# Layer 0 of a graph network on Trainium2: the next layer's projection moved between weighing and y2's product, and y1 transposed from its two parts

## The chip, the core and the metric

The kernel runs on one core of a Trainium2 chip. The metric is the time of the whole program on the device in microseconds (us). Its median of three runs before the change is 1384.36 us (1383.07 to 1384.51).

## What is computed

Four layers with residual and layer normalisation over x of shape (8, 2048, 64) and a 2048 x 2048 matrix `adj` whose rows are 0 or one constant. The change concerns layer 0 and the first step of layer 1:

```python
# layer 0
w = einsum('nd,dkio->nkio', embedding, weight)      # 16 x 3 x 64 x 64 weight, one mix per node
As = [I, A, 2 A A - I]                              # K = 3
x_g = einsum('knm,bmc->bnkc', As, x)
out = einsum('bnki,nkio->bno', x_g, w) + embedding @ bias
x = layernorm(x + out)
# layer 1, first steps
h = x @ W
s = leaky_relu(h @ a_node, 0.2)
alpha = softmax(where(H.T > 0, s, NEG))
agg = einsum('ben,bnf->bef', alpha, h)
... x @ W_ind ...                                   # the other half of the projection
```

## The kernel before

The 2048 nodes are 16 tiles of 128; a tile holds 128 nodes by 512 columns (8 batches by 64 features). A stage ahead of layer 0 computes y1 = A x for all tiles and keeps it as two parts, `y_hi` (rounded to fp32r) and `y_lo` (the rest), because two fp32r products replace a full fp32 one.

`layer0` then runs a loop over j = 0 to 16, with eight groups g in each pass. The order on each engine is the order in which the code is written: `program_order` ties the instructions of PE (TensorE), DVE (VectorE), ACT (ScalarE) and POOL (GpSimd) one behind the other. The steps of a pass are:

- `weigh(j, g)` (L1010): PE multiplies the transposed terms x, y1, y2 of tile j with a slice of the weights into a tile `pp` of PSUM, 24 instructions; DVE drains it in four steps (L1031), which scale by the embedding and add to the residual `r`. The pool `ps_p` holds two such tiles, so weigh g needs that DVE has drained weigh g-2.
- `normed(j-1, 0..2)` (L1035) at g = 0, 1, 2: layer normalisation of the tile before, on DVE and ACT.
- `scaled(j+1, h)` (L931) and `compare` (L946): POOL and DVE check the mask of the next tile against the matrix; `mask(j+2, h)` makes the masks of the one after.
- `first_terms(j+1)` (L953) at g = 2: POOL adds `y_hi` and `y_lo` to y1 (L956); PE transposes it in four pieces with the identity (L959, listed under the helper's line L152); ACT copies the result. Then the bias product `bp` and the residual.
- `product(j+1)` (L978) at g = 3: y2's product, 32 matmuls with the mask. Behind it `to_features(j-1)` transposes the normalised tile to `xT1` (`trx`).
- `second_term(j+1)`, `scores(j-1)` and `gather(j-2)` at g = 6; the gather adds to `aggp` the product of `mds` (memberships) and `hss` (projected features times scores).
- `degrees(j+1)` (`dgp`, L1005) and `project(j-1)` (L1091) at g = 7. The projection takes a `pp` tile too (named `hp`): 8 products (16 instructions on PE), two ACT copies (L1115, L1116), a DVE subtraction (L1117) and POOL's product `hs` (L1124). It ends a pass, and the next instruction of PE is weigh(j+1, 0).

Pass 16 has no weighing left: it finishes tile 15, gathers tile 14, spreads the memberships over four SBUF tiles (`spread`, L1131), sums the softmax denominators (`denp`, L1144, 16 products) and gathers tile 15. Several tiles live in the homes (numbered buffers) of a pool `own`, which the stage before has left.

Of the kernel before, what the change touches and what calls it, by code (L numbers as in the profile page):

```python
# [8 lines left out]
F32 = mybir.dt.float32  # L9
# [37 lines left out]
def r_(ap):  # L47
    return ap.bitcast(F32R)
# [3 lines left out]
def kernel(  # L52
# [31 lines left out]

    ident = const.tile([P, P], F32, tag="ident", name="ident")
    make_identity(nc, ident)
    ones = const.tile([P, P], F32, tag="ones", name="ones")
    nc.vector.memset(ones, 1.0)
    eps_t = const.tile([P, 1], F32, tag="eps", name="eps_t")
# [61 lines left out]
    def transpose(dst, src):  # L151
        nc.tensor.matmul(dst, src, ident, start=True, stop=True, is_transpose=True)  # L152
# [727 lines left out]
    def layer0(  # L880
# [7 lines left out]
        raws, msk, terms, resid, norm, srow = {}, {}, {}, {}, {}, {}  # L888
        x1s, xTs, hps, hss, mds = {}, {}, {}, {}, {}

        homes = {"xT": (0, 1, 2), "xs": (3, 4), "y1": (5,), "y1T": (6, 7), "r": (8, 9),
                 "y2": (10,), "y2T": (11, 12), "cs": (13, 14), "sq": (15,)}
        turn = {}

        def tile(tag, name, shape=(P, BC), bufs=2):
            if tag not in homes:
                return l0s.tile(list(shape), F32, tag=tag, name=name, bufs=bufs)
            turn[tag] = turn.get(tag, -1) + 1
            home = homes[tag][turn[tag] % len(homes[tag])]
            return own.tile(list(shape), F32, tag=f"b0_{home}", name=name)  # L900
# [51 lines left out]

        def first_terms(j):  # L953

            y1 = tile("y1", f"y1_{j}")
            nc.gpsimd.tensor_tensor(y1, y_hi[:, j, :], y_lo[:, j, :], ALU.add)  # L956
            tr = ps_tr.tile([P, NP, P], F32, tag="tr", name=f"try1_{j}")
            for pr in range(NP):
                transpose(tr[:, pr, :], y1[:, pr * P:(pr + 1) * P])  # L959
            y1T = tile("y1T", f"y1T_{j}", (P, NP, P))  # L960
            nc.scalar.copy(y1T, tr)
            terms[j]["y1"] = y1T
            bp = ps_tr.tile([P, QW], F32, tag="tr", name=f"bp_{j}")
            nc.tensor.matmul(bp[:, 0:C], terms[j]["et"], bias_sb, start=True, stop=True)
            bn = tile("bn", f"bn_{j}", (P, C))
            nc.scalar.copy(bn, bp[:, 0:C])
            r = tile("r", f"r0_{j}")
            for bq in range(2):
                nc.gpsimd.tensor_tensor(
                    r[:, 4 * bq * C:4 * (bq + 1) * C]  # L970
                    .rearrange("p (h l c) -> p h l c", h=2, l=2),
                    swapped(terms[j]["xs"], bq),
                    bn.rearrange("p (h l c) -> p h l c", h=1, l=1).to_broadcast([P, 2, 2, C]),
                    ALU.add,
                )
            resid[j] = r
# [114 lines left out]
        def project(j):  # L1091

            mm = ps_p.tile([P, 2, 2, 4 * C], F32, tag="pp", name=f"hp_{j}")
            mm = mm.rearrange("p h l (m x) -> p h (l m) x", m=2)
            for pr in range(NP):
                for h in range(2):
                    rs = slice(h * 64, (h + 1) * 64)
                    nc.tensor.matmul(  # L1098
                        mm[:, h, pr, :], xTs[j][rs, pr, :], wb[rs], start=True, stop=True
                    )  # L1100
            if j < NT - 1:
                md = tile("md", f"md_{j}", (P, 2, E))
                nc.gpsimd.tensor_copy(md, pm[:, j, :].unsqueeze(1).to_broadcast([P, 2, E]))
                mds[j] = md.rearrange("p h e -> p (h e)")

            def by_half(t):
                return t.rearrange("p (r h c) -> p h r c", h=2, c=C)


            stay = j >= len(kept_i)  # L1110
            if stay:
                hi, lo = y_hi[:, j, :], y_lo[:, j, :]
            else:
                hi, lo = (tile(k, f"{k}_{j}", bufs=1) for k in ("ihi", "ilo"))
            nc.scalar.copy(r_(by_half(hi)), mm[:, :, :, C:2 * C])  # L1115
            nc.scalar.copy(by_half(h_sb[:, j, :]), mm[:, :, :, 0:C])  # L1116
            nc.vector.tensor_tensor(  # L1117
                r_(by_half(lo)), mm[:, :, :, C:2 * C], by_half(hi), ALU.subtract
            )
            if not stay:  # L1120
                for t, kept_part in zip((hi, lo), kept_i[j]):
                    nc.sync.dma_start(kept_part, t)
            hss[j] = tile("hs", f"hs_{j}", bufs=1)
            nc.gpsimd.tensor_tensor(  # L1124
                b_view(hss[j]), b_view(h_sb[:, j, :]), bcast(es[:, j, :]), ALU.mult
            )

        def gather(j):
            nc.tensor.matmul(aggp, mds[j], hss[j], start=j == 0, stop=j == NT - 1)  # L1129

        def spread():  # L1131

            mds.clear()
            for q, home in enumerate((1, 2, 3, 5)):
                md = own.tile([P, 4, 2, E], F32, tag=f"b0_{home}", name=f"md4_{q}")
                nc.gpsimd.tensor_copy(
                    md, pm[:, 4 * q:4 * q + 4].unsqueeze(2).to_broadcast([P, 4, 2, E])
                )
                for t in range(4):
                    mds[4 * q + t] = md[:, t].rearrange("p h e -> p (h e)")  # L1140

        def denominators(lo, hi):
            for j in range(lo, hi):
                nc.tensor.matmul(  # L1144
                    denp[0], mds[j], es[:, j, :], start=j == 0, stop=j == NT - 1
                )
# [19 lines left out]
        with program_order():  # L1166
            first_terms(0)
            scaled(0, 0)
            scaled(0, 1)
            for _ in product(0):  # L1170
                pass
            second_term(0)
            for j in range(NT + 1):
                first = j == 0
                if not first:
                    when(j + 2, load_adj)
                when(j + 2, load_x)
                for g in range(8):
                    when(j, weigh, g)
                    if g == 0:  # L1180
                        when(j - 1, normed, 0)
                        if first:
                            compare(0, 0)
                            compare(0, 1)
                            load_adj(2)
                    elif g == 1:
                        when(j - 1, normed, 1)
                        if j == NT:
                            denp.append(ps_acc.tile([P, BC], F32, tag="acc", name="denp")[:, 0:B])
                            gather(NT - 2)  # L1190
                            spread()
                            denominators(0, NT - 1)
                        if first:
                            degrees(0)
                        when(j + 1, scaled, 0)
                    elif g == 2:
                        when(j - 1, normed, 2)
                        when(j + 1, first_terms)
                    elif g == 3:
                        if j + 1 < NT:  # L1200
                            for _ in product(j + 1):
                                pass
                        when(j - 1, to_features)
                        when(j + 1, compare, 0)
                        when(j + 1, scaled, 1)
                        if j == NT - 2:
                            for t in range(len(kept_i)):
                                for y, kept_part in zip((y_hi, y_lo), kept_i[t]):
                                    nc.sync.dma_start(y[:, t, :], kept_part)
                        when(j + 2, mask, 0)  # L1210
                        when(j + 2, mask, 1)
                    elif g == 5:
                        when(j + 1, compare, 1)
                        if j:
                            next(flags, None)
                    elif g == 6:
                        when(j + 1, second_term)
                        when(j - 1, scores)
                        if j < NT:
                            when(j - 2, gather)  # L1220
                        else:
                            denominators(NT - 1, NT)
                            nc.vector.tensor_scalar(rden, denp[0], TINY, None, op0=ALU.max)
                            nc.vector.reciprocal(rden, rden)
                    elif g == 7:
                        when(j + 1, degrees)
                        when(j - 1, project)
            gather(NT - 1)


# [811 lines left out]
```

## Time and profile before

| what | busy us | share of the span |
|---|---|---|
| PE | 1308.3 | 95% |
| PEld (weight loads, overlapping PE) | 1025.6 | 74% |
| DVE | 929.7 | 67% |
| POOL | 442.3 | 32% |
| ACT | 363.8 | 26% |

| stage | from, us | to, us |
|---|---|---|
| y1's product | 7 | 150 |
| layer 0's loop | 150 | 742 |
| layer 1 | 742 | 1062 |
| layers 2 and 3 | 1062 | 1384 |

How to read the profile: a line of the timeline gives the start, the duration of a merged group of like instructions, the engine, the line of the kernel, the operation, the tile written and those read, the shape and the count; square brackets give how long the engine stood idle before it and which work released it. A line of waits gives who waited for whom, the total in us, how often, and the longest. An "issue" is time in which an engine waited for nothing that the profile shows. An fp32 matmul appears as two instructions; fp32r as one.

### The profile page before, as it was taken

Reading aid. Unit: us, or ns where it says so; the run is one execution under the profiler, and the core shown is the slowest. Engines: PE = TensorE matmul, PEld = TensorE weight load, DVE = VectorE, ACT = ScalarE, POOL = GpSimd, SP = SyncE. Lnnn points to the kernel's source line nnn. Section 1 sums busy time; section 2 is a strip of 40 time slices with the busy share of each in tenths; the row PEclk is TensorE's granted clock in tenths of the full one; section 3 lists DMA queues with packets and bytes.
Section 4 is the critical chain, followed back from the end, with each engine's and each line's share of the span. In section 5 each row is a group of like instructions: output and inputs, shape, how many; then the busy total and the mean of one; then the engine's idle time right before and its main releaser. Section 6 shows DMA issues by size and latency. Waiting matters only on the chain.

```text
span 1383.9 us, 19824 instructions
## 1 busy us (share of the span) xinstructions
PE 1308.3 (95%) x7692; PEld 1025.6 (74%) x7692; DVE 929.7 (67%) x1658; ACT 363.8 (26%) x844; POOL 442.3 (32%) x372
## 2 busy tenths in 40 slices
PE   7999889999999999999986799999997899999997
PEld 6777678888888888888875466666665688888885
DVE  5555347787777777777672678888885666566554
ACT  3000101212222111211221346665655321111111
POOL 0000443444444444444410345665653320000000
PEclk9999989999999999999995599999999899999999
DMA  9765323333323333221603121222220223333552
GB/s 311 215 184 173 128 95 102 102 102 102 99 93 98 103 102 101 98 98 62 218 27 114 61 79 75 76 77 76 77 76 1 92 72 116 117 122 138 184 188 71
DMA packets 91047, 153.00 MB, mean 111 GB/s; under 512 B 12097, under 2 KB 55489, under 8 KB 84673
## 3 DMA queue, kind: packets, MB, share of 16 engines
q1 hardware_dynamic: 88642, 147.46, 31.7%
q10 hardware_dynamic: 2304, 4.20, 0.8%
q8 instruction: 63, 1.03, 0.3%
q14 instruction: 38, 0.31, 0.1%
HBM read 115.97 MB, written 35.66 MB: 110 GB/s over the span
## 4 chain that ended last, share of the span: by engine, by line
PE 81%; DVE 3%; issue 2%; ACT 1%; POOL 1%; POOLq 0%; ACTq 0%; DVEq 0%
PE pp L1020 24%; PE a L1288 17%; PE ind L1288 9%; PE y2p L983 9%; PE fc L798 2%; PE u L1371 2%; PE df L807 2%; PE gp L693 2%; PE try L152 1%; PE yp L1400 1%; PE aggp L1129 1%; PE trm L152 1%; PE tr_l L152 1%; DVE r L1031 1%; PE hp L1098 1%
## 5 line engine op out<-in xcount | busy, mean ns | idle before, releaser
L1031 DVE SCALAR_TENSOR_TENSOR r<-pp,emb_sb,r 128x256 f32<-128x256 f32 x512 | 247.3, 483 | 134.3 <-PE pp L1020 119.7
L1020 PE MATMUL pp<-w_sb,xT 64*128 64x256 f32 x1024 | 163.1, 391 | 11.8 <-PE hp L1098 10.3
L1020 PE MATMUL pp<-w_sb,y1T 64*128 64x256 f32 x1024 | 156.7, 378 | 0.0
L1020 PE MATMUL pp<-w_sb,y2T 64*128 64x256 f32 x1024 | 156.6, 378 | 0.0
L1020 PEld LDWEIGHTS pp<-w_sb,xT 64*128 64x128 f32 x1024 | 98.2, 187 | 34.6 <-issue 15.1
L469 PE MATMUL y1p<-x_hi,m 128*128 128x512 f32 x256 | 106.2, 415 | 7.2 <-ACT x_hi L417 7.2
L734 POOL TENSOR_TENSOR ez<-ez,coef 128x1024 f32<-128x1024 f32 x32 | 65.1, 2033 | 141.2 <-DVE ez L732 141.2
L1020 PEld LDWEIGHTS pp<-w_sb,y1T 64*128 64x128 f32 x1024 | 104.1, 188 | 7.8
L1020 PEld LDWEIGHTS pp<-w_sb,y2T 64*128 64x128 f32 x1024 | 104.1, 188 | 7.9
L1288 PE MATMUL ind<-y_hi,mj_l 128*128 128x512 f32 x256 | 106.6, 417 | 1.0 <-DVE dlt L763 0.8
L983 PE MATMUL y2p<-y_hi,msk 128*128 128x512 f32 x256 | 103.7, 405 | 0.0
L1288 PE MATMUL a<-y_hi,mj_l 128*128 128x512 f32 x256 | 102.4, 400 | 0.0
L983 PE MATMUL y2p<-y_lo,msk 128*128 128x512 f32 x256 | 101.7, 397 | 0.0
L1288 PE MATMUL a<-y_lo,mj_l 128*128 128x512 f32 x256 | 101.6, 397 | 0.0
L469 PE MATMUL y1p<-x_lo,m 128*128 128x512 f32 x256 | 101.4, 396 | 0.0
L1288 PE MATMUL ind<-y_lo,mj_l 128*128 128x512 f32 x256 | 101.1, 395 | 0.0
L1288 PE MATMUL a<-v_hi,mj_l 128*128 128x512 f32 x256 | 100.1, 392 | 0.0
L1288 PE MATMUL a<-v_lo,mj_l 128*128 128x512 f32 x256 | 100.0, 391 | 0.0
L1124 POOL TENSOR_TENSOR hs<-h,es 128x512 f32<-128x512 f32 x16 | 16.7, 1044 | 246.3 <-ACT h L1116 222.3
L935 POOL TENSOR_TENSOR ms<-msk,srow 128x1024 f32<-128x1024 f32 x32 | 77.4, 2420 | 7.5 <-DVE ms L948 5.3
L1288 PEld LDWEIGHTS ind<-y_hi,mj_l 128*128 128x128 f32 x256 | 48.6, 190 | 33.7 <-issue 19.1
L948 DVE SCALAR_TENSOR_TENSOR ms<-ms,adj 128x1024 f32<-128x1024 f32 x32 | 63.9, 1998 | 0.0
(262 smaller groups left out, 2434.3 us busy)
## 6 DMA issues: line engine op xcount, KB each, us to landing
mj_l<-mask SPq DMA_DIRECT2D x48, 1024.0 KB, 4.9
raw<-in_at SPq DMA_DIRECT2D x32, 512.0 KB, 4.8
adj<-in_at SPq DMA_DIRECT2D x64, 256.0 KB, 3.3
mask<-msk SPq DMA_DIRECT2D x32, 512.0 KB, 3.1
xraw<-in_xn SPq DMA_DIRECT2D x8, 512.0 KB, 5.4
oh<-oh SPq DMA_DIRECT2D x16, 256.0 KB, 3.4
xT<-in_xt SPq DMA_DIRECT2D x16, 256.0 KB, 2.9
xs<-in_xn SPq DMA_DIRECT2D x16, 256.0 KB, 2.6
```

What stands on the lines that cost most here:

```text
L152: nc.tensor.matmul(dst, src, ident, start=True, stop=True, is_transpose=True)
L469: nc.tensor.matmul(accs[q][jj], r_(m[:, t, jj * P:(jj + 1) * P]), r_(part[:, mt, :]), start=i + h + t == 0 and part is x_hi, stop=i == 3 a ...
L693: nc.tensor.matmul(gp[:, u, :], r_((oh01, oh23)[i][rs, cols]), r_(part[rs]), start=part is agg_hi, stop=part is agg_lo,)
L734: nc.gpsimd.tensor_tensor(by_b(ez), by_b(ez), per_b(coef, 2 * i, 2), ALU.mult)
L798: nc.tensor.matmul(fc[:, h, :], fcw_sb[rs], sT[rs], start=True, stop=True)
L807: nc.tensor.matmul(df[:, b:b + 1], th[:, b % 2, (b // 2) * P:(b // 2 + 1) * P], av_sb, start=True, stop=True,)
L935: nc.gpsimd.tensor_tensor(ms, m, srow[j].unsqueeze(1).to_broadcast([P, 8, P]), ALU.mult)
L948: nc.vector.scalar_tensor_tensor(ms, ms, 1.0, raws[j][h], op0=ALU.mult, op1=ALU.not_equal, accum_out=bad[:, 2 * j + h:2 * j + h + 1],)
L983: nc.tensor.matmul(acc, r_(msk[j, mt // 8][:, mt % 8, :]), r_(part[:, mt, :]), start=mt == 0 and part is y_hi, stop=mt == NT - 1 and part ...
L1020: nc.tensor.matmul(pp[:, h, pl, :], terms[j][name][rs, 2 * bq + pl], w_sb[rs, k, dq * 4 * C:(dq + 1) * 4 * C], start=k == 0, stop=k == K - 1,)
L1031: nc.vector.scalar_tensor_tensor(rb, ppv[:, :, dd, :], emb_sb[:, j, d:d + 1], rb, op0=ALU.mult, op1=ALU.add)
L1288: nc.tensor.matmul(acc, r_(a[:, mt, :]), r_(part[:, mt, :]), start=mt == 0 and part is hi, stop=mt == NT - 1 and part is lo,)
```

## The change

The projection of tile j-2 is now issued at g = 3, after weigh(j, 3) and ahead of y2's product, instead of the projection of tile j-1 at the end of the pass. It is meant to have its PSUM tile drained while the product runs. In pass 16 the projection of tile 14 comes at g = 3, that of tile 15 after the loop, and gather(14) moves from g = 1 to g = 6, behind the last denominators. `hss` therefore lives in home 5, which y1 leaves, and `spread` uses home 10 in place of 5; in the last two projections the membership tile is taken from `spread`.

y1 is no longer summed by POOL: PE multiplies each of the two parts with a rounded identity and adds both in PSUM, 8 products of 128 x 128 by 128 in fp32r instead of 4 transposes in fp32.

```diff
     make_identity(nc, ident)
+    ident_r = const.tile([P, P], F32, tag="ident_r", name="ident_r")
+    nc.vector.tensor_copy(r_(ident_r), ident)
...
-        homes = {"xT": (0, 1, 2), "xs": (3, 4), "y1": (5,), "y1T": (6, 7), "r": (8, 9),
+        homes = {"xT": (0, 1, 2), "xs": (3, 4), "hs": (5,), "y1T": (6, 7), "r": (8, 9),
...
         def first_terms(j):
-            y1 = tile("y1", f"y1_{j}")
-            nc.gpsimd.tensor_tensor(y1, y_hi[:, j, :], y_lo[:, j, :], ALU.add)
             tr = ps_tr.tile([P, NP, P], F32, tag="tr", name=f"try1_{j}")
             for pr in range(NP):
-                transpose(tr[:, pr, :], y1[:, pr * P:(pr + 1) * P])
+                for part in (y_hi, y_lo):
+                    nc.tensor.matmul(
+                        tr[:, pr, :], r_(part[:, j, pr * P:(pr + 1) * P]), r_(ident_r),
+                        start=part is y_hi, stop=part is y_lo,
+                    )
...
-            if j < NT - 1:
+            if j not in mds:
                 md = tile("md", f"md_{j}", (P, 2, E))
...
-            for q, home in enumerate((1, 2, 3, 5)):
+            for q, home in enumerate((1, 2, 3, 10)):
...
                         if j == NT:
                             denp.append(ps_acc.tile([P, BC], F32, tag="acc", name="denp")[:, 0:B])
-                            gather(NT - 2)
                             spread()
                             denominators(0, NT - 1)
...
                     elif g == 3:
+                        when(j - 2, project)
                         if j + 1 < NT:
                             for _ in product(j + 1):
                                 pass
...
                             denominators(NT - 1, NT)
+                            gather(NT - 2)
                             nc.vector.tensor_scalar(rden, denp[0], TINY, None, op0=ALU.max)
...
                     elif g == 7:
                         when(j + 1, degrees)
-                        when(j - 1, project)
+            project(NT - 1)
             gather(NT - 1)
```

## The prediction

> **What bounds the kernel now.** I read the page's busy shares and its chain first, then PE's waits in layer 0 (200 to 740 us), then the timeline of one pass.
>
> ```profile
> PE 1308.3 (95%) x7692; PEld 1025.6 (74%) x7692; DVE 929.7 (67%) x1658; ACT 363.8 (26%) x844; POOL 442.3 (32%) x372
> ...
> PE 81%; DVE 3%; issue 2%; ACT 1%; POOL 1%; POOLq 0%; ACTq 0%; DVEq 0%
> ```
>
> TensorE sets the time: it is 95% busy and carries 81% of the chain that ended last. An edit counts by what it does to PE's queue. What PE waits for in layer 0:
>
> ```profile
> PE pp L1020 <- PE hp L1098: 10.3, 13, 0.8
> ...
> PE pp L1020 <- DVE r L1031: 1.4, 2, 1.1
> ```
>
> The first is one wait of 0.79 us in each of 13 passes, put down to the projection `hp`. The timeline, PE first, then DVE:
>
> ```profile
> 446.90 0.38 PE L1005 MATMUL dgp<-ones,cs 128*128 128x1 f32 x2
> 447.21 1.16 PE L1098 MATMUL hp<-wb,xT 64*128 64x128 f32 x16
> 449.16 0.70 PE L1020 MATMUL pp<-w_sb,xT 64*128 64x256 f32 x4 [0.79 <-PE hp L1098]
> ```
>
> ```profile
> 447.02 2.04 DVE L1031 SCALAR_TENSOR_TENSOR r<-pp,emb_sb,r 128x256 f32<-128x256 f32 x4 [1.56 <-PE pp L1020]
> 449.57 0.69 DVE L1117 TENSOR_TENSOR ilo<-hp,ihi 128x512 fp32r<-128x512 f32 x1 [0.51 <-ACT h L1116]
> ```
>
> `hp` is done by 448.37, yet weigh(j+1, 0) starts at 449.16, 0.10 after DVE has drained weigh 7 at 449.06. `pp` has two buffers and `hp` takes one of them (weigh 6's), so weigh(j+1, 0) must wait for weigh 7's. The releaser is DVE, not `hp`. A pass takes 35.07 us from one degree product to the next; in it DVE is busy 26.5 us (busy time by window), so DVE is second.
>
> [...] the trace has 108 to 109 ns between loads. [...] the comparison (L948) takes 3.00 us while GpSimd is at work, 1.22 us while it is idle.
>
> **The change part by part.**
>
> *The projection's place.* Same matmuls, ACT copies and DVE subtraction. At pass end, weigh(j+1, 0) now follows the degree product at 447.21 and takes weigh 6's buffer, which DVE released at 444.6: the wait is gone. At the new place, after weigh 3, `hp` takes weigh 2's buffer. PE's 1.2 us for `hp` are added there and leave the pass end: sum nothing. Behind it in PE's queue stands y2's product (32 matmuls), which uses no `pp`; the copies and the subtraction (0.59 + 0.59 + 0.69) lie under its 7.45 us. Weigh 5, which needs `hp`'s buffer, is some 10 us later. So gone are 13 x 0.79 = 10.3 us, plus 1.1 at 237 us (the first such pass, booked under DVE): **-11.4 us**.
>
> *Does another wait take its place?* With weigh(j+1, 0) at 447.21 and 2.6 us per weigh: weigh 1 at 449.87 needs weigh 7's buffer (449.06: free); weigh 2 at 452.47 needs weigh 0's (matmuls done 450.1, drained 2.04 us later, 452.15: free by 0.3); weigh 3 at 456.8 needs weigh 1's (normed's 1.4 us stand between, so 455.6: free); `hp` at 459.5 needs weigh 2's (458.1: free). None, but the slack at weigh 2 is small. On DVE the subtraction now precedes the comparison and two masks (at most 3.0 + 2.9 us), ahead of weigh 4's drain; DVE stood idle 2.96 us before that drain, and `hp` gives PE 1.2 us more, so it is hidden.
>
> *GpSimd.* `hs` no longer keeps scaled(j+1, 0) waiting 14.79 us for ACT; the sum of y1 (1.27 us, L956) goes. It ended at 422.02 and the transposes began at 422.07, so at most 0.05 us per pass was on the path; I count nothing. `hs` now delays scaled(j+1, 1) by about 2 us; its user, the comparison, comes 15.4 us after the product's start: hidden.
>
> *y1's transposes.* Per pass 4 transposes become 8 fp32r products of 128x128 by 128. Before, 4 take 0.59 us to the next operation:
>
> ```profile
> 422.07 0.66 PE L152 MATMUL try<-ident,y 128*128 128x128 f32 x4
> 422.66 0.43 PE L964 MATMUL bp<-bias_sb,et 16*128 16x64 f32 x2
> ```
>
> They start 0.11 us apart. No run of them in fp32r is in the trace, but a single one of the same shape is, between 512-column products:
>
> ```profile
> 144.07 0.19 PEld L390 LDWEIGHTS sm<-S,rk 128*128 128x128 f32 x1
> 144.30 0.22 PE L390 MATMUL sm<-S,rk 128*128 128x128 f32 x1
> 144.36 0.45 PE L469 MATMUL y1p<-x_hi,m 128*128 128x512 f32 x1
> ...
> 144.64 0.39 PE L469 MATMUL y1p<-x_lo,m 128*128 128x512 f32 x1
> ```
>
> From 144.30 to 144.64 are 0.34 us, where one product alone takes 0.23: the short one costs 0.11, a weight load. I take 0.11. The lower bound is 0.06 (the distance to its successor), the upper 0.23 (a 512-column product). At 0.11: 4 more x 0.11 = 0.44 per pass, x 15 = **+6.6 us** (upper: 8 x 0.23 - 0.44 = 1.4, x 15 = 21). The first tile's are at 150.5 us at half clock (4 took 1.08): +0.85, of which 0.45 falls into the bias product's wait for a DMA: **+0.4**.
>
> *End of the layer.*
>
> ```profile
> 719.40 1.06 PE L1098 MATMUL hp<-wb,xT 64*128 64x128 f32 x16
> 722.75 1.13 PE L1129 MATMUL aggp<-hs,md 128*128 128x512 f32 x2 [2.29 <-POOL hs L1124]
> 723.72 6.17 PE L1144 MATMUL denp<-es,md 128*128 128x8 f32 x30
> 729.74 1.09 PE L152 MATMUL trx<-ident,x 128*128 128x128 f32 x4
> ...
> 735.28 0.60 PE L1144 MATMUL denp<-es,md 128*128 128x8 f32 x2 [1.42 <-ACT es L1089]
> ```
>
> The gather, queued ahead of the denominators, waits 2.29 us for `hs`. Afterwards the denominators start at 719.7 (`md` is spread early: its homes are free) and, still at full clock (0.11 each), end at 723, the projection of tile 14 at 724.3. Then trx waits for x1 of tile 15, which comes at 726.5 (before 727.2; the 0.69 us subtraction is no longer ahead): 3.2 us earlier than 729.74. But gather(14) now stands behind the last denominator and ahead of the last projection: 2.05 us at half clock (as L1129 at 740.18), 1.03 at full. I take half and round up for the extra copies and the table loads: **-1.7** here (-0.7 to -2.7; were all at full clock, some -3).
>
> *Small.* The copy of the identity lies in DVE's first wait for a load (3.79 us): nothing. The chain for `dinv` (L1324 on), which DVE works off at 693 to 696 while it waits, would hold up weigh 0's drain about 0.9 us in one pass, more than the slack of 0.3: **+0.4**. Layers 1 to 3 are untouched.
>
> Sum: -11.4 + 6.6 + 0.4 - 1.7 + 0.4 = -5.7, so 1384.4 - 5.7 = **1378.7 us**.
>
> **The rivals.** (a) *A wait in the place of the old one.* DVE's drain (2.04 us a weigh plus normed) becomes what ends last at weigh 2 or 3, and the loop keeps its 35.07 us. For: the slack of 0.3, and PE already waited 0.32 once (703.06). Against: DVE has 8 us free in a pass. Only the end of the layer gains: 1384.4 + 0.4 - 1.7 = 1383.1. (b) *The short products are dear.* At 0.23 each: -11.4 + 21 + 1 - 1.7 + 0.4 = +9.3, 1393.7, slower. For: they have never been run back to back here. Against: L390's 0.11, in 12 of its 16 places. (c) *The end gains more*, if the clock holds through the last scores and gathers: some 3 us more than in the sum, 1375.7.
>
> **How the numbers follow.** My case 0.62, (a) 0.14, (b) 0.08, (c) 0.16. The time is the first's. The range reaches (c) and (a) and a price of 0.16 for a short product (+0.05 x 8 x 15 = 6): 1374.5 to 1384.5. 0.2% is 2.8 us: my case and (c) are faster, less a part of my case in which a slightly higher price leaves under 2.8: faster 0.76, same 0.15, slower 0.09.
>
> **What would show it.** Right: passes of about 34.75 us; no wait of `pp` at pass ends; `hp` starting 0.3 us after weigh 3; the eight short products in about 0.9 us; `aggp` last ending about 1.7 us earlier against the end of weigh(15, 7). Wrong: a wait of `pp` on DVE at weigh 1 to 3, the short products above 0.15 us apart, y2's product waiting behind `hp`, or the comparison taking 3.0 us where it took 1.22.

## The result, and the profile after

The changed kernel takes 1367.32 us (median of four runs), the kernel before beside it 1383.80 us: ratio 0.9878, 95% interval 0.9859 to 0.9897. The gain is 16.5 us, where 5.7 were predicted and 1374.5 was the low end of the range. One of the four runs (1393.83) had a lower clock (0.946, against 0.966 to 0.968 in the others) and is not in the ratio. The profiled executions stand 19.8 us apart (spans 1383.9 and 1364.1), 3.3 us more than the medians: the one before took 1385.91 us, 2.1 above its median, the one after 1366.07, 1.25 below. The stages below are from these two, one execution each.

The page of the kernel after: busy shares, and shares of the chain that ended last.

```profile
PE 1306.2 (96%) x7756; PEld 1021.9 (75%) x7756; DVE 929.9 (68%) x1659; ACT 364.5 (27%) x844; POOL 420.4 (31%) x355
...
PE 83%; DVE 3%; ACT 1%; issue 1%; POOL 0%; ACTq 0%; POOLq 0%; DVEq 0%
```

PE still sets the time and has hardly less to do (1308.3 us busy before); what went is time in which it waited, as the stages below show. PE's waits in layer 0 after (160 to 735 us), with the lines that answer to those of before:

```profile
PE aggp L1133 <- POOL hs L1128: 2.3, 1, 2.3
PE pp L1024 <- DVE r L1035: 1.7, 3, 1.1
```

The 13 waits of `pp` put down to `hp` are gone. The timeline of PE after, at a pass's end and at the projection's new place:

```profile
435.76 0.38 PE L1009 MATMUL dgp<-ones,cs 128*128 128x1 f32 x2
436.07 0.70 PE L1024 MATMUL pp<-w_sb,xT 64*128 64x256 f32 x4
...
447.71 0.60 PE L1024 MATMUL pp<-w_sb,y2T 64*128 64x256 f32 x4
448.14 1.06 PE L1102 MATMUL hp<-wb,xT 64*128 64x128 f32 x16
449.13 0.50 PE L987 MATMUL y2p<-y_hi,msk 128*128 128x512 f32 x1
```

Weigh 0 follows the degree product after 0.31 us, `hp` follows weigh 3 without a gap, and y2's product starts 0.99 us after `hp`. So far it is as the prediction had it. Where the 19.8 us went is seen when layer 0 is cut at its degree products (`dgp`, from the trace). That of tile 0 stands in pass 0 behind weigh 1, each of the others at the end of a pass; so what is called the first pass here is pass 0 from its third weigh on. "Last weighing" is the start of its last matmul, "`agg`" the start of the first step of layer 1 on DVE:

| stage | before, us | after, us | difference |
|---|---|---|---|
| start to the first degree product | 168.95 | 169.48 | +0.53 |
| from it to the second (first pass of the loop) | 34.23 | 26.18 | -8.05 |
| second to third | 32.13 | 32.60 | +0.47 |
| third to fourth | 35.39 | 34.45 | -0.94 |
| the next twelve passes | 421.68 | 414.10 | -7.58 |
| last degree product to the last weighing | 26.81 | 27.07 | +0.26 |
| last weighing to `agg`, the first step of layer 1 | 23.10 | 20.55 | -2.55 |
| layers 1 to 3 | 641.59 | 639.69 | -1.90 |

The largest single piece, 8.05 us, lies in a stretch in which the moved projection has no part: the first projection came at 235.6 us before. Three timelines of the kernel before show what stood there. First POOL:

```profile
169.81 3.27 POOL L935 TENSOR_TENSOR ms<-msk,srow 128x1024 f32<-128x1024 f32 x1 [5.30 <-DVE ms L948]
173.04 1.27 POOL L939 TENSOR_TENSOR cs<-msk 128x512 f32<-128x512 f32 x1
174.39 0.72 POOL L940 TENSOR_TENSOR cs<-cs 128x256 f32<-128x256 f32 x1
175.19 0.45 POOL L941 TENSOR_TENSOR cs<-cs 128x128 f32<-128x128 f32 x1
175.60 1.26 POOL L956 TENSOR_TENSOR y<-y_hi,y_lo 128x512 f32<-128x512 f32 x1
```

then PE, and last the comparison on DVE that POOL waited for:

```profile
176.92 1.11 PE L152 MATMUL try<-ident,y 128*128 128x128 f32 x4 [4.80 <-POOL y L956]
```

```profile
168.51 1.22 DVE L948 SCALAR_TENSOR_TENSOR ms<-ms,adj 128x1024 f32<-128x1024 f32 x1
```

POOL's scaled(1, 0) needs an `ms` buffer, and DVE frees one only with compare(0, 0), which in the first pass stands behind the drain of weigh 0. The sum of y1 is queued behind scaled(1, 0), and PE's transposes, with everything behind them, wait 4.80 us for that sum. The short products do not need it: after the change PE goes from weigh 2 into them without a wait.

```profile
172.58 0.33 PE L960 MATMUL try<-ident_r,y_hi 128*128 128x128 f32 x1
```

### The profile page after: what moved, and what is told of

Its sections match the earlier page's. It is cut to its first block, busy times and chain, and to the rows that moved or that the text cites. A ratio compares the mean times of both kernels' runs of the same rounds, so it can differ in the third digit from the quotient of the medians.

```text
span 1364.1 us, 19987 instructions
## 1 busy us (share of the span) xinstructions
PE 1306.2 (96%) x7756; PEld 1021.9 (75%) x7756; DVE 929.9 (68%) x1659; ACT 364.5 (27%) x844; POOL 420.4 (31%) x355
## 4 chain that ended last, share of the span: by engine, by line
PE 83%; DVE 3%; ACT 1%; issue 1%; POOL 0%; ACTq 0%; POOLq 0%; DVEq 0%
PE pp L1024 24%; PE a L1293 17%; PE ind L1293 9%; PE y2p L987 9%; PE fc L800 3%; PE u L1376 2%; PE df L809 2%; PE gp L695 2%; PE trm L154 1%; PE yp L1405 1%; PE try L960 1%; PE aggp L1133 1%; PE tr_l L154 1%; PE sgp L1081 1%; PE dp L720 1%
## 5 line engine op out<-in xcount | busy, mean ns | idle before, releaser
L1024 PE MATMUL pp<-w_sb,y1T 64*128 64x256 f32 x1024 | 153.5, 376 | 0.0
L1024 PE MATMUL pp<-w_sb,y2T 64*128 64x256 f32 x1024 | 153.5, 376 | 0.0
L973 POOL TENSOR_TENSOR r<-xs,bn 128x256 f32<-128x256 f32 x32 | 22.6, 727 | 412.2 <-issue 262.7
L1024 PEld LDWEIGHTS pp<-w_sb,xT 64*128 64x128 f32 x1024 | 94.4, 186 | 25.1 <-issue 14.9
L1024 PEld LDWEIGHTS pp<-w_sb,y1T 64*128 64x128 f32 x1024 | 99.7, 187 | 10.9
L1024 PEld LDWEIGHTS pp<-w_sb,y2T 64*128 64x128 f32 x1024 | 99.6, 187 | 11.0
L937 POOL TENSOR_TENSOR ms<-msk,srow 128x1024 f32<-128x1024 f32 x32 | 89.9, 2809 | 5.6 <-DVE ms L950 5.6
L929 DVE TENSOR_SCALAR msk<-adj 128x1024 fp32r<-128x1024 f32 x32 | 63.7, 2024 | 4.1 <-PE y1p L471 4.1
```

Of the source, the lines that this page charges most:

```text
L929: nc.vector.tensor_scalar(r_(m), raws[j][h], 0.0, None, op0=ALU.is_gt)
L937: nc.gpsimd.tensor_tensor(ms, m, srow[j].unsqueeze(1).to_broadcast([P, 8, P]), ALU.mult)
L1024: nc.tensor.matmul(pp[:, h, pl, :], terms[j][name][rs, 2 * bq + pl], w_sb[rs, k, dq * 4 * C:(dq + 1) * 4 * C], start=k == 0, stop=k == K - 1,)
```

## The experiments

The kernel before was run again beside each experiment. Its medians there were 1385.67, 1385.89 and 1385.44 us, not 1383.80, and the ratios below are against these runs. The theory after the result: (T1) the first pass was held up by POOL's sum, by the wait and by a half clock of PE after it; (T2) the move gains what the drained buffer gains, somewhat more than the wait shown; (T3) the short products cost what was predicted. The rivals: the move shortens the first pass too; the half clock comes by itself; the short products cost nothing, or more.

**The move alone.** The changed kernel, with y1 as before:

```diff
+            y1 = tile("y1", f"y1_{j}")
+            nc.gpsimd.tensor_tensor(y1, y_hi[:, j, :], y_lo[:, j, :], ALU.add)
...
-                for part in (y_hi, y_lo):
...
+                transpose(tr[:, pr, :], y1[:, pr * P:(pr + 1) * P])
```

> The projection moved as in the change, y1 summed on POOL and transposed in fp32 as before. My theory after the result: the first pass of layer 0 (34.2 us from one degree product to the next before, 26.2 after) was held up by POOL's sum of y1, which is in this kernel again; so the first pass stays at 34 us with a wait of 4.8 us for POOL, later passes take 35.07 - 1.06 = 34.0 us (no wait at pass ends), and the end of the layer gains 2 to 3 us: 1366 to 1369 us. The rival, that the move itself shortens the first pass, expects 26 us there and about 1360 us. The prediction's own terms (11.4 us of waits, 1.7 at the end) give 1370.7.

Measured: 1367.88 us, ratio 0.9871 (0.9855 to 0.9888). Later passes take 34.00 us, and the wait in the first pass is still there:

```profile
PE try L152 <- POOL y L956: 4.8, 1, 4.8
```

So the move doesn't remove it, and the rival falls. The first pass takes 32.66 us all the same, 1.57 less than before with the same wait: the half clock after it (granted clock 0.50) lasts 6.8 us here, 10.2 before. That part of the gain can't be put down to the moved projection, which comes later. The move alone gains as much as the whole change, as far as the two intervals can tell.

**y1 alone.** The kernel before with the short products; the projection stays at the pass's end.

```diff
-            y1 = tile("y1", f"y1_{j}")
-            nc.gpsimd.tensor_tensor(y1, y_hi[:, j, :], y_lo[:, j, :], ALU.add)
...
-                transpose(tr[:, pr, :], y1[:, pr * P:(pr + 1) * P])
+                for part in (y_hi, y_lo):
...
```

> Only y1's transposes by short products; the projection stays at the end of the pass (hs in home 5, spread in home 10, for room). My theory: the first pass falls to about 26.2 us with PE at full clock, each later pass costs 0.42 us more (35.5), pass-end waits of 0.79 us stay: 1383.8 - 8 + 6.5 = 1382 to 1383 us. The rival, that the first pass was shortened by the move, expects 34.6 us there and 1390 us. If a short product cost 0.23 us: 36.4 us per pass and about 1396.

Measured: 1382.27 us, ratio 1.0007 (0.9971 to 1.0042), with runs from 1381.47 to 1400.10: no difference that this can tell. The stages show why it is small: the first pass takes 26.18 us, as after the change, and later passes 35.51, 0.44 more than before. Of the 8.05 us the later passes give 6.2 back. The profiled execution is 3.0 us shorter than that of before (span 1380.9); 1.7 of these lie between the last weighing and `agg` (21.41 us), where the order of work was not edited.

**The sum earlier.** The kernel before with POOL's sum at g = 0, ahead of scaled:

```diff
                     if g == 0:
+                        when(j + 1, y1_sum)
                         when(j - 1, normed, 0)
```

`y1_sum` is the sum, taken out of `first_terms`; that of tile 0 stands ahead of the loop.

> The kernel before with one edit: POOL sums y1 of the next tile at the start of a pass, ahead of scaled, so that it does not stand behind POOL's wait for DVE in the first pass. My theory: the wait of 4.8 us goes and the clock stays full, so the first pass takes 25.8 us, the others 35.07: 1375 us. The rival, that the half clock in that pass comes by itself, expects only the 4.8 us: 1379 us, with the half clock still there. If the sum was not what held the transposes, 1383.8.

Measured: 1379.57 us, ratio 0.9944 (0.9925 to 0.9962). The first pass falls to 25.72 us, 8.51 less, and its half clock is gone: the four transposes take 0.66 us, 1.11 before, and follow weigh 2 without a wait:

```profile
172.64 0.66 PE L152 MATMUL try<-ident,y 128*128 128x128 f32 x4
```

T1 is borne out, in the pass. The median is 6.1 us below that of the kernel before beside it, where 8.8 were expected. In the trace the stage from the last weighing to `agg` takes 24.24 us (23.10 before) and layers 1 to 3 643.37 (641.59). Nothing was edited there; the stretches of half clock lie elsewhere (from 714.5 us on, 724.0 before).

**The wait filled.** The kernel before, with 18 products that nobody reads in PE's queue ahead of the first pass's transposes:

```diff
+                        if first:
+                            full = ps_tr.tile([P, QW], F32, tag="tr", name="fill")
+                            for _ in range(18):
+                                nc.tensor.matmul(
+                                    full, r_(msk[0, 0][:, 0, :]), r_(y_hi[:, 0, :]),
...
```

> The kernel before, with 18 products ahead of the first pass's transposes of y1 that nobody reads (4.1 us of PE in the time in which it waits for POOL). The wait's length stays, PE does not idle in it. My theory, that idle PE brings half clock for the next 10.24 us and so costs about 5 us: the transposes start when they did, the clock stays full, the pass takes about 29.2 us, 1379 us. The rival (the clock drops whatever PE does there): 34.2 us and 1384 us.

Measured: 1382.15 us, ratio 0.9973 (0.9964 to 0.9982). The transposes start 8.06 us after the degree product, as before (7.97); the pass takes 30.68 us, 3.55 less. The busy time by window, from 174.4 to 184.7 us, first before, then here (PE, PEld, DVE, ACT, POOL; then the granted clock, the DMA share and GB/s):

```profile
174.40:184.70 10.30, 7.78 (x32) 5.72 (x33) 1.09 (x4) 0.80 (x2) 8.04 (x8) 0.50 0.16 46
```

```profile
174.40:184.70 10.30, 9.76 (x57) 7.59 (x56) 4.20 (x9) 0.70 (x2) 8.54 (x9) 1.00 0.24 71
```

The transposes wait as long, PE isn't idle meanwhile (busy for 9.76 of the 10.30 us, 7.78 before), and the clock holds (1.00, 0.50 before): in this pass the half clock comes from the idle PE. So of the 8.5 us that the sum cost, 3.6 are the clock and some 5 the wait (4.80 by its line). The expected 5 us for the clock were too many, since PE stands still in 2.5 of the 10.3 us.

**Move, early sum, no short products.** The first experiment and the early sum together:

> The move, without the short products: y1 is transposed in fp32 as before, and POOL sums it at the start of a pass. My theory adds the parts up: first pass 25.7 us (as with the early sum alone), later passes 34.0 (as with the move alone), against 26.2 and 34.43 after the change: 15 x 0.43 = 6.5 us less than the change, 1360 us, give or take 2 for where the half-clock stretches of layer 1 fall. The rival, that the short products cost nothing in the changed kernel because they lie in time that PE has to spare, expects the change's 1367.

Measured: 1360.49 us, ratio 0.9805 (0.9747 to 0.9863). First pass 25.72, later passes 34.00, as added up: the short products do cost 0.43 us a pass in the changed kernel, and the rival falls.

**The last gather.** At the end of the layer, gather(14) ahead of the last denominators; first on top of the kernel just shown, then on top of the change.

```diff
+                            gather(NT - 2)
                             denominators(NT - 1, NT)
-                            gather(NT - 2)
```

> As b1_move_early_sum, and at the end of the layer gather of tile 14 stands ahead of the last denominators, in PE's wait of 1.42 us for es. My theory: from the last weighing to agg 1.4 us less (20.55 to 19.1), 1358 to 1359 us. The rival: the gather holds up the last denominators and nothing is gained.

> The changed kernel with only gather of tile 14 ahead of the last denominators. My theory: the 2.05 us that it takes behind them fall to 0.6, the end of the layer from 20.55 to about 19.1 us, 1365.5 us. The rival: no difference, 1367.

Measured: 1358.43 us, ratio 0.9792 (0.9743 to 0.9841), all runs between 1357.94 and 1359.46 where those without the edit lie between 1359.60 and 1360.71; and 1366.45 us on top of the change, which its total does not tell from 1367.32. From the last weighing to `agg` it takes 19.7 us in both, against 21.50 and 20.55. PE at the end of the first of the two:

```profile
708.36 2.06 PE L1133 MATMUL aggp<-hs,md 128*128 128x512 f32 x2
710.21 0.42 PE L1343 MATMUL badp<-bad,ones 128*128 128x1 f32 x2
710.49 0.57 PE L1148 MATMUL denp<-es,md 128*128 128x8 f32 x2
```

The gather lies in what was a wait for `es`. The 20.55 of the change held 3.4 us at full clock near its end, from 721.0 us on (its last gather takes 1.12 us, 2.08 in these two and in the first one's base), so the 1.78 of the first pair is the nearer comparison; that the clock is the same throughout in that pair is not shown. The kernel with the move, the early sum and the earlier gather is the fastest: 8.0 us below the change with the earlier gather, on the same chip.

**Another place for the projection.** After weigh 1, between two weighs; first with y1 summed on POOL, then with the short products.

```diff
                     elif g == 1:
+                        when(j - 2, project)
                         when(j - 1, normed, 1)
...
                     elif g == 3:
-                        when(j - 2, project)
```

> The projection of tile j-2 after weigh 1, between two weighs, where no long product lies ahead; y1 as before the change. My theory (what counts is that PE has work without a pp tile while DVE drains): hp takes weigh 0's buffer, weigh 2 must wait for weigh 1's drain, which stands behind normed on DVE; passes of 35.0 to 36.5 us with a wait of pp on DVE at weigh 2. The rival (only leaving the pass end counts, next to the degree product): 34.0 us as with the move.

> The changed kernel (y1 by short products, no sum on POOL) with the projection of tile j-2 after weigh 1, as in e6_between_weighs. My theory: of the 9.6 us per pass that the place between two weighs cost there, only the wait for DVE's drain at weigh 2 (2.0 us) and its clock-free remainder belong to the place; the rest is POOL's sum of y1, queued behind hs, with the half clock that follows the wait. Without the sum: 34.4 + 2.1, passes of 36.5 to 37 us, about 1400 us. The rival, that the place itself costs it all: passes of 43 to 44 us, 1490 us.

Measured: 1493.68 us, ratio 1.0768 (1.0705 to 1.0831), passes of 42.0 to 44.5 us, 43.1 on average; and 1413.7 us, ratio 1.0218 (1.0188 to 1.0248), passes of 36.75 us, but five of the thirteen longer by 1.7. PE's waits in layer 0 in the first:

```profile
PE try L152 <- POOL y L956: 41.8, 14, 4.8
PE pp L1020 <- DVE r L1031: 28.5, 14, 2.1
```

and in the second:

```profile
PE pp L1024 <- DVE r L1035: 28.5, 14, 2.1
PE denp L1148 <- POOL md L1140: 6.1, 1, 6.1
```

The wait of 2.0 us for DVE's drain came at weigh 2 as expected, so leaving the pass's end is not enough: what counts is PE work without a `pp` tile behind the projection. The expectation of 35 to 36.5 us for the first failed by 7 us. There `hs`, which waits for ACT, stands in POOL's queue ahead of scaled and of the sum:

```profile
458.52 1.04 POOL L1124 TENSOR_TENSOR hs<-h,es 128x512 f32<-128x512 f32 x1 [26.81 <-ACT h L1116]
```

PE waits for the sum as in the first pass, 13 times more (2.3 to 4.4 us each), and the granted clock from 200 to 700 us is 0.91 on average, where it is 1.00 in the kernel before. Without the sum that part is gone, as expected. The total of 1400 left out two things: the 6.1 us that the last denominators wait for `md`, queued behind `hs` as well, and the clock in the five longer passes. The clock records of the trace change in steps of 3.41 us. In those five passes the wait of 2.03 us lies wholly within one step, and the next step is at half clock (0.50); in the other eight it is spread over two steps, and the clock stays full (1.00). An example of each (columns as above):

```profile
306.87:310.29 3.42, 1.40 (x21) 1.23 (x21) 3.28 (x7) 2.26 (x4) 0.61 (x1) 1.00 0.09 37
310.29:313.70 3.41, 3.41 (x19) 3.25 (x18) 0.75 (x2) 0.91 (x2) 3.41 (x3) 0.50 0.33 122
269.33:272.74 3.41, 1.89 (x26) 1.63 (x22) 3.26 (x7) 1.48 (x3) 0.00 (x0) 1.00 0.00 0
272.74:276.15 3.41, 2.90 (x25) 2.60 (x26) 1.55 (x4) 1.69 (x3) 3.22 (x2) 1.00 0.42 155
```

## Why the prediction was wrong

The direction and the mechanism at the pass's end were right, the size was not. By its own steps:

1. *"At most 0.05 us per pass was on the path; I count nothing"* (POOL's sum of y1). **This step failed.** It was read off the pass at 420 us and taken for all. In the first pass the sum ended 4.80 us too late and brought 10.2 us of half clock: 8.5 us together, as the early sum shows. The profile of before held this wait, at 176.92; the prediction's list of waits begins at 200 us, behind it, and no later pass stands for the first one.
2. *"Gone are 13 x 0.79 = 10.3 us, plus 1.1."* Right mechanism, mis-sized. Passes fell by 1.07 us (35.07 to 34.00 with the move alone); the passes behind the first gained 13.9 us with the move alone, where 11.0 were predicted, `dinv` included. The sizes follow from the starts of the instructions. Before, weigh 0 started 2.26 us after the degree product (446.90 to 449.16), after the change 0.31: 1.95 less. At its new place `hp` adds 0.89: y2's product starts 1.42 us after the last line of weigh 3 (447.71 to 449.13), and 0.53 where no `hp` stands between. That leaves 1.06. The 0.79 is idle time, counted from the end of `hp`'s last matmul; but matmuls overlap (records of 0.27 us, pairs 0.11 apart), so that a weigh that needn't wait starts before that end.
3. *"At 0.11: 4 more x 0.11 = 0.44 per pass"* (the short products). Right: 34.44 against 34.00 us. (A product in fp32r is one instruction, and so was each transpose: `try` x4 before.) The trace after has them 0.11 us apart:

```profile
444.21 0.28 PE L960 MATMUL try<-ident_r,y_lo 128*128 128x128 f32 x1
444.32 0.28 PE L960 MATMUL try<-ident_r,y_hi 128*128 128x128 f32 x1
444.43 0.28 PE L960 MATMUL try<-ident_r,y_lo 128*128 128x128 f32 x1
```

4. *"Does another wait take its place?"* *"None"*. Right for passes 2 to 14. Pass 15 has no y2 product behind `hp`, and there weigh 4 waits 1.06 us for DVE's drain of weigh 3:

```profile
691.47 0.70 PE L1024 MATMUL pp<-w_sb,xT 64*128 64x256 f32 x4 [1.06 <-DVE r L1035]
```

   With the two waits behind the `dinv` chain (0.64 us; 0.4 was predicted) pass 15 came out 0.26 us longer instead of 1.07 shorter.
5. *The first tile, +0.4:* measured +0.53, which shows nothing: the stage took 168.7 to 170.0 us in kernels without the short products. *The end, -1.7:* measured -2.55, inside the -0.7 to -2.7 given. The step that gather(14) ends up on the path was right:

```profile
716.46 0.60 PE L1148 MATMUL denp<-es,md 128*128 128x8 f32 x2 [1.42 <-ACT es L1093]
716.91 2.06 PE L1133 MATMUL aggp<-hs,md 128*128 128x512 f32 x2
```

   The size is in part luck: with the old order at the end the stage took from 21.41 us (y1 alone) to 24.24 (the early sum), with the half clock in different places (from 714.5 us on in the early sum, 724.0 before).
6. *"Layers 1 to 3 are untouched", 0:* measured -1.9, in one execution each. They were not edited. The half-clock stretch at `agg` ends 46.5 us behind it before and is 44.4 us long after, which explains some 1.1 us, by an estimate (half of the 2.1 us between them); the rest was not tried. Nineteen runs of the kernel before, unedited, lie between 1383.67 and 1387.18 us, so this is no effect of the change that can be told.

The sum, by stage: 0.5 for the first tile, -8.05 in the first pass, -7.8 in the others (where -4.4 was predicted, `dinv` included), -2.55 at the end, -1.9 behind it. That is 14.1 us more than the 5.7 predicted: some 8.5 are the failed step, 2.9 the size of the waits at the pass's end, 0.9 the end of the layer and 1.9 the layers behind it. The small slack at weigh 2, which made rival (a), held.

## What to carry to other kernels

Read the waits of the first and the last pass by themselves: buffers fill and queues stand differently there, and one wait of 4.8 us on the engine that sets the time cost 8.5 with the clock it lost. Before an operation is moved from an engine with time to spare to the busiest one, see whether it can be issued earlier in its own queue: here that saved the same wait without 0.43 us a pass. In this kernel a further user of the double buffer belonged ahead of a stretch in which PE works without that buffer, and the pass that lacks the stretch had to be costed apart. And the gain of a removed wait is better taken from starts, with and without it, than from the idle time shown (1.07 us here against 0.79).

## What the runs showed of the hardware

The same wait of PE, 4.8 us at nearly the same place, was followed by 10.2 us of half clock in the kernel before and by 6.8 in the move alone. In the traces before and after, every stretch of half clock (0.50) that ends within the trace is a multiple of 3.41 us: 3.41, 6.83, 10.24, 13.65, 44.37 and 64.85. The filled wait, with PE busy for 9.76 of 10.30 us instead of 7.78, kept the clock at 1.00. How long PE has to be idle for the clock to fall is not shown, but in the second kernel with the projection between weighs it fell without a step that was idle throughout: PE was busy for 1.40 of 3.42 us, and the next 3.41 us were at 0.50, while the same wait of 2.03 us spread over two steps (1.89 and 2.90 us busy) left it at 1.00. So here the price of a wait depended on where it fell: passes with it in one step took 1.7 us longer.

What had not been expected is how far stages that nobody edited differ: layers 1 to 3 took between 639.7 and 646.4 us in the eleven traces, one for each kernel, with the same order of work. The two longest, the early sum (643.4) and the filled wait (646.4), have the most half clock behind `agg` (80.2 and 83.2 us, 69.9 to 75.2 in the others); that this is all of it is not shown. A difference of some 2 us between totals of such kernels is better read from the stages than from the totals.
